# A recommender forward pass: the last block's first layer begun in the counts' PSUM banks, transposes tile by tile, token rows that drift against the counts, and tables split by TensorE

## The chip, the cores and the metric

The kernel runs on one core of one Trainium2 chip. A core has five engines that work side by side, each through its own instructions in order: TensorE (PE, matrix products and transposes into PSUM), VectorE (DVE), ScalarE (ACT), GpSimd (POOL, which here issues the gathers) and SyncE (SP, plain transfers). The metric is the device time in microseconds of one execution. In tables and profiles, PEld is TensorE's loading of weights, which overlaps PE.

## The reference

There are 16384 examples. Each has 32 token indices into a table of 50000 rows of 300 numbers, three lists of 20 indices into smaller tables (1000, 5000 and 10000 rows of 64) and four single indices (tables of 100, 50, 20 and 1000 rows of 64). Rows are averaged or taken, put side by side to 748 features, and passed through three dense layers; a "wide" sum of one number per small index is added at the end.

```python
tok = word_emb[token_idx].mean(axis=1)                 # 32 rows of 300
e1 = emb_mh1[mh1_idx].mean(axis=1)                     # 20 rows of 64; e2, e3 alike
o1 = emb_oh1[oh1_idx]                                  # o2, o3, o4 alike
emb = concatenate([tok, e1, e2, e3, o1, o2, o3, o4], axis=1)
wide = (wide_mh1[mh1_idx].sum(axis=(1, 2)) + ... + wide_oh4[oh4_idx][:, 0])[:, None]
h = relu(emb @ W1 + b1)      # 748 -> 1024
h = relu(h @ W2 + b2)        # -> 512
h = relu(h @ W3 + b3)        # -> 256
return sigmoid(h @ Wd + bd + wide)
```

## The kernel before

The batch is cut into 128 tiles of 128 examples. A tile's **token rows** are gathered by POOL with indirect transfers, one row per example and transfer, 32 transfers a tile, two to a buffer (a "group"); DVE adds them into a sum that lives in PSUM. The sums over the **small tables** are matrix products: for each tile DVE makes one-hot rows, TensorE multiplies them into counts (how often an example uses each of the 128 x 138 table rows), ScalarE moves the counts to SBUF as 8-bit numbers, and TensorE multiplies the counts with the tables, which are held on the chip as three bf16 terms. A tile takes 11 steps of counting; the small sums of tile t run in the steps of tile t + 1. The layers of a block of four tiles (512 examples) are spread over the steps of the next four tiles.

```python
tokp = ctx.enter_context(tc.tile_pool(name="tok", bufs=2 * TOK_LAG))       # TOK_LAG = 3
ps_h = ctx.enter_context(tc.tile_pool(name="ps_h", bufs=2, space=bass.MemoryType.PSUM))
ps_c = ctx.enter_context(tc.tile_pool(name="ps_c", bufs=1, space=bass.MemoryType.PSUM))
... # tables: each part of 23 slices becomes three bf16 terms
            for c in range(3):
                ...
                if c:
                    nc.vector.scalar_tensor_tensor(
                        rows, rows, 2.0 if c == 1 else 1.0, term[c - 1], op0=ALU.mult, op1=ALU.subtract
                    )
                nc.scalar.activation(term[c], rows, AF.Copy, scale=2.0 if c == 0 else 1.0)
                yield 1
... # token rows
    def add_up(t, q, rows):
        a, b = rows[:, 0:TOK_D], rows[:, TOK_D : 2 * TOK_D]
        if q == 0:
            nc.vector.tensor_add(tok_sum, a, b)
        else:
            nc.vector.tensor_add(tok_sum, tok_sum, a)
            to = features[t][:, 0:TOK_D] if q == n_groups - 1 else tok_sum
            nc.vector.tensor_add(to, tok_sum, b)

    def tokens(t, it):
        for q in range(n_groups):
            rows = tokp.tile([P, TOK_GROUP * TOK_D], F32, name="tok_rows")
            for r in range(TOK_GROUP):
                j = q * TOK_GROUP + r
                nc.gpsimd.indirect_dma_start(...)
            under_way.append((t, q, rows))
            if len(under_way) > TOK_LAG:
                add_up(*under_way.pop(0))
            yield 1
... # small sums: by pairs of tables
                    nc.tensor.matmul(
                        pg[:, j, :], by_slice[:, :, h], terms[:, h, :], start=(h == h0), stop=(h == h1 - 1)
                    )
... # features transposed for the layers, 512 examples at a time
    def transposed(x, gs):
        n = len(gs) * P
        for k in range(NK):
            kk = chunk_k[k]
            pt = ps_h.tile([P, BLOCK], F32, name="pt", tag="ph")
            for s, g in enumerate(gs):
                nc.tensor.transpose(pt[:kk, s * P : (s + 1) * P], chunk(g, k), ident)
            nc.vector.tensor_scalar(
                x[:kk, k, 0:n], pt[:kk, 0:n], scale[:kk, k : k + 1], None, ALU.mult
            )
            yield CHUNK_WORK
... # one layer: n_out groups of matmuls, each ended by one ScalarE operation
            ph = ps_h.tile([P, BLOCK], F32, name="ph", tag="ph")
            for k, kk in enumerate(kks):
                nc.tensor.matmul(ph[:, 0:n], weights[:kk, k, m * P : (m + 1) * P], src[:kk, k, 0:n], ...)
            nc.scalar.activation(dst[:, m, 0:n], ph[:, 0:n], AF.Relu, bias=bias[:, m : m + 1])
... # order of the whole
    sizes = [NSUB] * (tiles // NSUB - 1) + [NSUB - 2, 1, 1]
    for t in range(tiles + 1):
        ...
        for i in range(STEPS):                       # 11 steps
            if t < tiles:
                hot = one_hots(...)                  # for the next step
                counts(cnt, hot_now, i)
                tables_on_chip.to(TABLE_PACE * (t * STEPS + i - 2))
                toks.to(n_groups * (i + 1) / STEPS)
            done = next(sums) if sums else 0
            if layers:
                layers.to(...)                       # its share of the step
```

Of the kernel before, what the change touches and what calls it, by code (L numbers as in the profile page):

```python
# [8 lines left out]
F32 = mybir.dt.float32  # L9
# [14 lines left out]
TOK_LAG = 3  # L24
BLOCK = 512
HALF = P // 2
N_SMALL = 3 * N_MH + 4
ONEHOT = 6
STEPS = -(-HALF // ONEHOT)
CHUNK_WORK = 1  # L30
TABLE_PACE = 1.2
LAYER_TIME = 10
# [6 lines left out]
G_COLS = TOK_D + 7 * ROW  # L39
# [7 lines left out]
def kernel(  # L47
# [23 lines left out]
    NSUB = BLOCK // P  # L71
# [5 lines left out]
    for f in SMALL:  # L77
# [4 lines left out]
    tokp = ctx.enter_context(tc.tile_pool(name="tok", bufs=2 * TOK_LAG))  # L82
    const = ctx.enter_context(tc.tile_pool(name="const", bufs=1))
    idxp = ctx.enter_context(tc.tile_pool(name="idx", bufs=2))
# [4 lines left out]
    gp = ctx.enter_context(tc.tile_pool(name="g", bufs=NSUB + 1))  # L89
    wp = ctx.enter_context(tc.tile_pool(name="wide", bufs=2 * NSUB))  # L90
    xp = ctx.enter_context(tc.tile_pool(name="x", bufs=1))
# [8 lines left out]
        [(0, 128)],  # L100
        [(128, 256)],
        [(256, 300), (684, 748)],
        [(300, 428)],
        [(428, 556)],
        [(556, 684)],
    ]
# [7 lines left out]
    scale = const.tile([P, NK], F32, name="scale")  # L114
    nc.vector.memset(scale, 1.0)
    nc.vector.memset(scale[:, 0:2], 1.0 / N_TOK)
    nc.vector.memset(scale[0 : TOK_D - 256, 2:3], 1.0 / N_TOK)
    nc.vector.memset(scale[:, 3:4], 1.0 / N_MH)
    nc.vector.memset(scale[0:EMB, 4:5], 1.0 / N_MH)
# [23 lines left out]
    PART = n_h // 6  # L143

    def load_tables(part0, tag):
        raw = xp.tile([P, PART, ROW], F32, name="raw", tag=tag)
# [14 lines left out]
    def convert_tables():  # L161


        tags = ("even", "odd")
        raws = [load_tables(k * PART, tags[k]) for k in range(2)]
        yield
        for part in range(n_h // PART):
            rows = raws[part]
            if 1 <= part < n_h // PART - 1:
                raws.append(load_tables((part + 1) * PART, tags[(part + 1) % 2]))  # L170
            for c in range(3):
                term = [
                    terms[:, part * PART : (part + 1) * PART, k * ROW : (k + 1) * ROW]
                    for k in range(3)
                ]
                if c:
                    nc.vector.scalar_tensor_tensor(
                        rows, rows, 2.0 if c == 1 else 1.0, term[c - 1], op0=ALU.mult, op1=ALU.subtract
                    )
                nc.scalar.activation(term[c], rows, AF.Copy, scale=2.0 if c == 0 else 1.0)  # L180
                yield 1
# [22 lines left out]
    under_way = []  # L204
    features = {}

    def add_up(t, q, rows):

        a, b = rows[:, 0:TOK_D], rows[:, TOK_D : 2 * TOK_D]
        if q == 0:  # L210
            nc.vector.tensor_add(tok_sum, a, b)  # L211
        else:
            nc.vector.tensor_add(tok_sum, tok_sum, a)  # L213
            to = features[t][:, 0:TOK_D] if q == n_groups - 1 else tok_sum
            nc.vector.tensor_add(to, tok_sum, b)  # L215

    def tokens(t, it):


        for q in range(n_groups):  # L220
            rows = tokp.tile([P, TOK_GROUP * TOK_D], F32, name="tok_rows")
            for r in range(TOK_GROUP):
                j = q * TOK_GROUP + r
                nc.gpsimd.indirect_dma_start(  # L224
                    out=rows[:, r * TOK_D : (r + 1) * TOK_D],
                    out_offset=None,
                    in_=word,
                    in_offset=bass.IndirectOffsetOnAxis(ap=it[:, j : j + 1], axis=0),
                )
            under_way.append((t, q, rows))  # L230
            if len(under_way) > TOK_LAG:
                add_up(*under_way.pop(0))
            yield 1

    def last_tokens():
        for group in under_way:
            add_up(*group)

    def load_indices(blk):
# [15 lines left out]
        return it, ix  # L255
# [309 lines left out]
```

## Time and profile before

| what | before |
|---|---|
| device time, median of 3 | 5270.46 us (5268.77 to 5272.05) |
| span of the profiled run | 5269.3 us |
| mean granted TensorE clock | 0.989 |
| gathers | 4096, busy 3896.4 us, 951 ns each |
| DVE busy | 3768.8 us |
| ScalarE busy | 2447.1 us |
| f32 matmuls of the layers (5984 records) | 1474.1 + 1211.0 us |
| small-table matmuls (17664) | 1849.6 us |
| counts (16384) | 758.4 us |

A line of the profile's list of groups gives source line, engine, operation, output and inputs by the program's names, how often, then busy time and mean length of one in ns, then the engine's idle time just before them and what ended it. A line of the timeline gives start and length in us, the same names, and in brackets the idle time before. In the names, `tok_rows` are gathered token rows, `own` is the PSUM bank with the token sum, `pc` the counts in PSUM, `cnt` the counts in SBUF, `pg` the small sums, `pt` transposes, `ph` a layer's output, `terms` the tables' bf16 terms and `raw` the tables as loaded. L224 is the gather, L388 a layer's matmul, L337 a small-table matmul, L312 a counting matmul, L177 the table subtraction. Busy time of an engine is the time in which an instruction of it is under way; what an engine spends between instructions is not in it.

### The profile page before, as it was taken

What the parts mean: (1) busy time and instruction counts of PE and PEld (TensorE: products, weight loads), DVE (VectorE), ACT (ScalarE), POOL (GpSimd) and SP (SyncE); (2) the same over time, 40 slices, a digit from 0 to 9 for tenths busy, and PEclk for the clock granted to TensorE, in tenths of its full rate; (3) what the DMA queues carried; (4) which work ended last, traced back from release to release, by engine and by line L of the source; (5) the groups of instructions that cost most, each with busy time, mean ns of one, the idle gap of its engine ahead of it and who ended that gap; (6) DMA issues with size and microseconds to landing.
All of it is one profiled execution on the core that took longest, in us unless ns stands there. A gap on an engine that the chain in (4) does not pass through costs nothing.

```text
span 5269.3 us, 104252 instructions
## 1 busy us (share of the span) xinstructions
PE 5094.7 (97%) x41320; PEld 3164.7 (60%) x41320; DVE 3768.8 (72%) x8014; ACT 2447.1 (46%) x1938; POOL 3897.3 (74%) x4103
## 2 busy tenths in 40 slices
PE   4799999999999999999999999999999999999999
PEld 3565656566565656656655656556566566656658
DVE  8777777777777777777777777777777777777752
ACT  5444444444444444444444444444444444444432
POOL 7777777777777777777777777777777777777762
PEclk8899999999999999999999999999999999999999
DMA  6444444444444444444444444444444444444431
GB/s 190 125 125 124 125 125 126 126 125 124 125 125 125 125 124 125 125 125 126 125 124 125 126 125 126 124 125 125 125 125 125 124 126 125 125 125 125 124 103 34
DMA packets 252890, 652.60 MB, mean 124 GB/s; under 512 B 119009, under 2 KB 119524, under 8 KB 252399
## 3 DMA queue, kind: packets, MB, share of 16 engines
q0 software_dynamic: 196608, 629.41, 43.5%
q1 hardware_dynamic: 55791, 16.53, 1.4%
q8 instruction: 323, 5.29, 0.4%
q14 instruction: 168, 1.38, 0.1%
HBM read 645.59 MB, written 0.07 MB: 123 GB/s over the span
## 4 chain that ended last, share of the span: by engine, by line
PE 37%; DMA 23%; DVE 16%; issue 14%; POOL 10%; ACT 0%; DVEq 0%; SPq 0%; POOLq 0%; ACTq 0%
DMA tok_rows<-in_word_emb_dram,it 22%; PE ph L388 20%; PE pg L337 12%; POOL tok_rows L224 10%; DVE own L215 5%; PE pc L312 4%; DVE own L213 3%; DVE slice L294 3%; DVE row L294 2%; DVE x L379 1%; DVE g L343 1%; PE po L413 1%; DVE own L211 0%; DVE g L215 0%; PE po L417 0%
## 5 line engine op out<-in xcount | busy, mean ns | idle before, releaser
L224 POOL DMA_INDIRECT tok_rows<-in_word_emb_dram,it x4096 | 3896.4, 951 | 1293.4 <-issue 755.5
L319 ACT ACTIVATE cnt<-pc 128x1656 fp8e3<-128x1656 f32 (+1 forms) x1408 | 2121.7, 1507 | 2056.4 <-PE pc L312 2026.0
L337 PE MATMUL pg<-terms,cnt 128*128 128x195 bf16 x17664 | 1849.6, 254 | 87.7 <-DVE g L343 86.3
L337 PEld LDWEIGHTS <-cnt 128*128 128x128 fp8e3 x17664 | 1601.3, 144 | 234.6 <-issue 81.1
L388 PE MATMUL ph<-x,w_sb 128*128 128x512 f32 (+5 forms) x3264 | 1474.1, 581 | 4.2 <-DVE x L379 3.5
L215 DVE TENSOR_TENSOR own<-own,tok_rows 128x300 f32<-128x300 f32 x1792 | 857.7, 479 | 680.6 <-DMA tok_rows<-in_word_emb_dram,it 647.3
L388 PE MATMUL ph<-h,w_sb 128*128 128x512 f32 (+2 forms) x2720 | 1211.0, 573 | 0.0
L213 DVE TENSOR_TENSOR own<-own,tok_rows 128x300 f32<-128x300 f32 x1920 | 918.8, 479 | 387.6 <-DMA tok_rows<-in_word_emb_dram,it 335.8
L312 PEld LDWEIGHTS <-row 64*128 64x128 bf16 x16384 | 501.7, 95 | 1041.3 <-DVE own L215 246.1
L294 DVE TENSOR_TENSOR row<-own,sc 128x768 bf16<-128x768 bf16 (+1 forms) x1408 | 762.4, 541 | 162.8 <-PE pc L312 89.5
L312 PE MATMUL pc<-slice,row 64*128 64x138 bf16 x16384 | 758.4, 224 | 70.6 <-DVE slice L294 36.7
L388 PEld LDWEIGHTS ph<-x,w_sb 128*128 128x128 f32 (+1 forms) x3264 | 564.3, 194 | 414.6 <-issue 401.9
L294 DVE TENSOR_TENSOR slice<-own,sc 128x828 bf16<-128x828 bf16 (+1 forms) x1408 | 797.9, 567 | 0.0
L388 PEld LDWEIGHTS ph<-h,w_sb 128*128 128x128 f32 x2720 | 463.3, 192 | 317.9 <-issue 316.0
L397 ACT ACTIVATE h<-ph,b_sb 128x512 f32<-128x512 f32 (+2 forms) x476 | 316.3, 665 | 683.2 <-PE ph L388 678.2
L343 DVE TENSOR_REDUCE g<-pg 128x130 f32<-128x390 f32 (+1 forms) x512 | 259.2, 506 | 151.1 <-PE pg L337 150.8
L379 DVE TENSOR_SCALAR x<-pt,scale 128x512 f32<-128x512 f32 (+4 forms) x204 | 137.0, 712 | 3.7 <-PE pt L378 2.9
L378 PE MATMUL pt<-ident,g 128*128 128x128 f32 (+1 forms) x768 | 104.1, 275 | 3.0 <-DVE x L379 2.5
L211 DVE TENSOR_TENSOR own<-tok_rows 128x300 f32<-128x300 f32 x128 | 61.4, 480 | 49.5 <-DMA tok_rows<-in_word_emb_dram,it 47.3
L378 PEld LDWEIGHTS pt<-ident,g 128*128 128x128 f32 (+1 forms) x768 | 85.5, 141 | 7.7 <-DVE x L379 6.7
L215 DVE TENSOR_TENSOR g<-own,tok_rows 128x300 f32<-128x300 f32 x128 | 60.2, 471 | 22.3 <-DMA tok_rows<-in_word_emb_dram,it 18.3
L413 PE MATMUL po<-h,wd_sb 128*1 128x512 f32 (+2 forms) x136 | 60.9, 566 | 0.3
(34 smaller groups left out, 290.1 us busy)
## 6 DMA issues: line engine op xcount, KB each, us to landing
tok_rows<-in_word_emb_dram,it POOLq DMA_INDIRECT x4096
ix<-in_idx_dram SPq DMA_DIRECT2D x128, 32.0 KB
w_sb<-in_W_dram SPq DMA_DIRECT2D x6, 512.0 KB
raw<-in_mh_dram SPq DMA_DIRECT2D x3, 747.5 KB
it<-in_idx_dram SPq DMA_DIRECT2D x32, 64.0 KB
w_sb<-in_W_dram SPq DMA_DIRECT2D x1, 2048.0 KB
raw<-in_mh_dram SPq DMA_DIRECT2D x1, 617.5 KB
out_dram<-h SPq DMA_DIRECT2D x31, 2.0 KB
```

The costliest lines, as they stand in the source:

```text
L213: nc.vector.tensor_add(tok_sum, tok_sum, a)
L215: nc.vector.tensor_add(to, tok_sum, b)
L224: nc.gpsimd.indirect_dma_start(out=rows[:, r * TOK_D : (r + 1) * TOK_D], out_offset=None, in_=word, in_offset=bass.IndirectOffsetOnAxis(ap ...
L294: nc.vector.tensor_tensor(one[:, 0:rows, :].rearrange("p i (n d) -> p i n d", d=2), iota[:, 0:n].rearrange("p (n d) -> p n d", d=2).unsque ...
L312: nc.tensor.matmul(pc[:, f, k // n, at : at + n_h], hot[0][half, k, :], hot[1][half, k, :], start=True, stop=True,)
L319: nc.scalar.activation(cnt[:, :, b : b + rows, :].rearrange("l f (g k) h -> l f g (k h)", g=2), pc[:, :, :, 0 : n * n_h], AF.Copy, scale=0 ...
L337: nc.tensor.matmul(pg[:, j, :], by_slice[:, :, h], terms[:, h, :], start=(h == h0), stop=(h == h1 - 1))
L343: nc.vector.tensor_reduce(g[:, at : at + n * ROW].rearrange("p (f d) -> p f d", f=n), pg[:, 0:n, :].rearrange("p f (c d) -> p f d c", c=3) ...
L378: nc.tensor.transpose(pt[:kk, s * P : (s + 1) * P], chunk(g, k), ident)
L379: nc.vector.tensor_scalar(x[:kk, k, 0:n], pt[:kk, 0:n], scale[:kk, k : k + 1], None, ALU.mult)
L388: nc.tensor.matmul(ph[:, 0:n], weights[:kk, k, m * P : (m + 1) * P], src[:kk, k, 0:n], start=(k == 0), stop=(k == len(kks) - 1),)
L397: nc.scalar.activation(dst[:, m, 0:n], ph[:, 0:n], AF.Relu, bias=bias[:, m : m + 1])
```

## The change

Five things change together. (1) The tables' second and third bf16 terms are no longer made by subtracting on DVE: TensorE adds the raw table and minus one half of the terms made so far in PSUM, seven slices at a time, and ScalarE copies the difference out. (2) Blocks of the layers hold two tiles (256 examples) and not four, with two blocks of one tile at the end. The features of a tile are transposed as soon as they are there: the small ones and the token sums each by themselves, into tiles of their own; the wide sum rides along as a row of one of the transposes and is added by DVE, where TensorE added it with a matmul per tile. (3) The token rows have one queue for the whole batch, spread over all steps and 16 more (WAKE), so that a tile's rows may come in later than its counts; there are eight buffers for them and not six. (4) For the last tile the part of the first layer that needs no token sum is done early for four of its eight outputs, in the PSUM banks which the counts no longer need. (5) The pacing follows: a block's layers are spread from when its features are ready until those of the next block will be.

```diff
-TABLE_PACE = 1.2
-LAYER_TIME = 10
+TOK_BUFS = 8
+WAKE = 16
+EARLY = 3
+LAYER_TILES = 2
+SPLIT = 7
+PART = 3 * SPLIT
+TABLE_PACE = 1.3
+LAYER_TIME = 2.5
...
+        def make(p, c):
+            if c == 0:
+                nc.scalar.activation(term(p, 0), rows(p), AF.Copy, scale=2.0)
+                return
+            _, a, b = pieces[p]
+            left = ps_h.tile([P, SPLIT, ROW], F32, name="left", tag="ph")[:, 0 : b - a, :]
+            nc.tensor.matmul(left, ident, rows(p), start=True, stop=False)
+            for k in range(c):
+                nc.tensor.matmul(left, minus_half, term(p, k), start=False, stop=(k == c - 1))
+            nc.scalar.activation(term(p, c), left, AF.Copy, scale=2.0)
...
+    n_all = B // P * n_groups + TOK_LAG
+    def tokens():
+        under_way = []
+        for n in range(n_all):
+            if n < n_all - TOK_LAG:
+                t, q = divmod(n, n_groups)
...
+            if n >= TOK_LAG:
                 add_up(*under_way.pop(0))
             yield 1
...
+        def add_small(self, t, g):
+            at = self.columns(t)
+            pt = ps_h.tile([P, 4, P], F32, name="pt", tag="ph")
+            nc.tensor.transpose(pt[:, 3, :], g[:, 0:P], ident)
+            for k in range(3):
+                c = (1 + 2 * k) * ROW + 1
+                nc.tensor.transpose(pt[:, k, :], g[:, c : c + P], ident)
+            nc.vector.tensor_tensor(self.small[:, 0:3, at], pt[:, 0:3, :], scale..., ALU.mult)
+            nc.vector.tensor_copy(self.small[0:EMB, 3, at], pt[0:EMB, 3, :])
+            nc.vector.tensor_copy(self.wide[:, at], pt[EMB : EMB + 1, 3, :])
+        def add_tokens(self, t, g):
...
+            for k in range(2):
+                nc.tensor.transpose(pt[:, k, :], g[:, k * P : (k + 1) * P], ident)
+            nc.tensor.transpose(pt[0 : EMB + rest, 2, :], g[:, TOK_D - rest - EMB : TOK_D], ident)
...
+    def early_part(block):
+        part = ps_c.tile([P, 4, 512], F32, name="pc")
+        for m in range(4):
+            for k in range(NK - 3):
+                nc.tensor.matmul(part[:, m, 0 : block.n], w1_sb[...], block.chunk(k), start=(k == 0), stop=False)
...
-        for s, wide in enumerate(wides):
-            nc.tensor.matmul(
-                po[:, s * P : (s + 1) * P], wide, ident, start=False, stop=(s == len(wides) - 1)
-            )
+        nc.vector.tensor_add(y, po[:, 0:n], block.wide[:, 0:n])
...
-    sizes = [NSUB] * (tiles // NSUB - 1) + [NSUB - 2, 1, 1]
+    n_steps = tiles * STEPS + WAKE
+    sizes = [LAYER_TILES] * (tiles // LAYER_TILES - 1) + [1] * LAYER_TILES
...
+        toks.to(n_all * (step + 1) / n_steps)
...
+        if step == n_steps - EARLY:
+            part = early_part(block_of[tiles - 1])
```

## The prediction

> **What bounds the kernel now.** I read the page's table of engines first: it points at TensorE (97% busy) and gives GpSimd 74%. The busy time by stage, read next (columns: stretch, its length, busy us and instructions of PE, PEld, DVE, ACT, POOL, then clock and DMA), says something else.
>
> ```profile
> PE 5094.7 (97%) x41320; PEld 3164.7 (60%) x41320; DVE 3768.8 (72%) x8014; ACT 2447.1 (46%) x1938; POOL 3897.3 (74%) x4103
> ```
>
> ```profile
> 100.00:125.00 25.00, 15.51 (x189) 13.04 (x187) 18.95 (x39) 12.17 (x8) 18.90 (x21) 0.84 0.46 124
> ...
> 2000.00:3000.00 1000.00, 985.36 (x7967) 601.91 (x7966) 730.89 (x1557) 468.69 (x367) 756.67 (x799) 0.99 0.46 125
> 3000.00:4000.00 1000.00, 986.01 (x7966) 602.21 (x7964) 727.62 (x1549) 469.25 (x368) 756.96 (x798) 0.99 0.46 125
> ```
>
> POOL does the same 798 or 799 gathers in every thousand microseconds, and about as many per us (21 in 25 us) before any layer runs and PE is a third idle. The timeline of POOL alone shows why: a gather starts every 1.25 us, 0.95 busy and 0.30 of its own overhead, whatever the view puts in brackets.
>
> ```profile
> 2499.57 0.95 POOL L224 DMA_INDIRECT tok_rows<-in_word_emb_dram,it  x1 [0.30 <-issue]
> 2500.82 0.95 POOL L224 DMA_INDIRECT tok_rows<-in_word_emb_dram,it  x1 [0.31 <-DVE own L213]
> 2502.07 0.95 POOL L224 DMA_INDIRECT tok_rows<-in_word_emb_dram,it  x1 [0.30 <-issue]
> ```
>
> So the gathers are the bound: 4096 x 1.2535 us (1000 us over 797.8) = 5134 us. The first starts at 3.1 us and the last ends at 5191.3, so POOL lost 5191.3 - 3.1 - 5134 = 54 us. Two places hold it. At the start, twelve table subtractions on DVE each hold one gather up; below, the gather that starts at 25.16 takes 2.09 us, because it can only proceed when the subtraction of 24.72 ends at 26.43.
>
> ```profile
> 24.72 1.71 DVE L177 SCALAR_TENSOR_TENSOR raw<-raw,terms 128x1495 f32<-128x1495 f32 x1
> ...
> 25.16 2.09 POOL L224 DMA_INDIRECT tok_rows<-in_word_emb_dram,it  x1 [0.30 <-issue]
> ```
>
> Twelve gathers are longer than 1.3 us, all so placed; together 11 us over 0.95 each. The rest, 43 us, falls after 5050 us: PE runs the two-tile block squeezed into one tile's steps, DVE follows PE, and gathers wait for buffers.
>
> ```profile
> 5153.54 0.95 POOL L224 DMA_INDIRECT tok_rows<-in_word_emb_dram,it  x1 [5.35 <-DVE g L215]
> ...
> 5163.70 0.54 PE L312 MATMUL pc<-slice,row 64*128 64x138 bf16 x12
> 5164.18 1.51 PE L337 MATMUL pg<-terms,cnt 128*128 128x195 bf16 x15
> 5165.53 3.65 PE L388 MATMUL ph<-x,w_sb 108*128 108x256 f32 x16
> 5169.11 0.54 PE L312 MATMUL pc<-slice,row 64*128 64x138 bf16 x12
> 5169.59 1.52 PE L337 MATMUL pg<-terms,cnt 128*128 128x195 bf16 x15
> 5170.94 4.08 PE L388 MATMUL ph<-x,w_sb 128*128 128x256 f32 x18
> ```
>
> A step there is 5.4 us (counts at 5163.70, then at 5169.11), the next 5.8, against 40.1 / 11 = 3.65 in the middle. After the last gather PE still works 78 us, to 5269.3: the rest of that block and two blocks of one tile. Thus 5269.3 = 3.1 + 5134 + 11 + 43 + 78.
>
> PE is the near second. In the middle a tile takes 32 x 1.2535 = 40.1 us, PE is busy 0.985 of it: 39.5 us. It begins the layers only after step 57, at 224 us.
>
> [...] POOL is full at 74 to 76%. [...] The trace has each f32 matmul as two records whose starts lie 429 ns apart at 512 columns, 216 at 256 and 112 at 128 (read in the tail)[...], and halving N costs almost nothing.
>
> **The change part by part.**
>
> *Tables split by TensorE.* Twelve DVE subtractions of 1.71 us go: POOL gets back 11 us. In their place PE does 40 f32 matmuls (ident x raw, 455 columns at most: 2 x 0.385 us) and 60 bf16 ones (about 0.2 us): 31 + 13 = 44 us within steps 3 to 19. ScalarE makes 60 terms of 455 columns instead of 18 of 1495; between 0.37 (128 columns) and 0.69 us (512) one takes about 0.63. Per step that is 1.3 pieces: PE 1.3 x 2.2 = 2.9, with counts (0.6) and, from step 11, sums (1.2) some 4.7 us; ScalarE 1.55 + 1.3 x 1.9 = 4.0. POOL's pace is 3.6. Over 17 steps the lag comes to 15 to 20 us, more while the clock is halved (the 0.84 above). Eight buffers less the lag of three let POOL run 12.5 us ahead, so I charge 8 us. Net gain at the start: 3 us.
>
> *Blocks of two tiles, transposed tile by tile.* The first ph matmul comes after 34 steps' counts instead of 57. Matmuls per tile: 88 records of 216.4 ns instead of 44 of 430: +0.13 us. Transposes 7 instead of 6 (+0.11), no wide matmuls (2 x 0.109 less), two more switches from f32 to bf16 (0.096 each, from 525 against 429 ns between starts): together +0.21, so 39.7 us a tile, all on PE's path. From the built order, PSUM banks are taken so that only 16 of 619 ph-after-ph reuses follow within 1 us; no new wait of size. DVE gains about 0.7 us a tile of small copies (75 to 80% busy, beside other work); ScalarE 0.48 us twice for 0.69: beside other work.
>
> *Drifting token rows.* The 2048 groups plus 3 are spread over 1424 steps instead of tile by tile over 1408: 1.4403 groups a step, 2.507 us each: 3.611 us a step, 39.7 a tile. POOL stays full, counts run ahead of it, and when the last row lands only one tile's layers are left. PE's need is 39.7 too: the two bounds meet, and PE has nothing to spare.
>
> *The end.* Block 124-125 gets 11 steps, then 126 alone, 127 begun early in the counts' banks. PE's built order, priced by start-to-start times of this trace (pg 0.0875, a switch from f32 0.096 more), leaves after step 1393: 308 pg 28 us, 128 f32 matmuls of 256 columns 57, 176 of 128 columns 40, counts 7, transposes and output 5: 137 us, the last block's 17.5 among them. By then DVE has added group 1.4403 x 1394 - 3 = 2005, which landed at about 3.1 + 2006 x 2.507 + 5.8 (1.25 issue, 4.5 in flight as the chain of waits shows) = 5038, with the 8 us above 5046. Then 137, layer-boundary bubbles of about 3, and 2.4 from the last matmul to the end (5266.9 to 5269.3 now): 5188. POOL alone would allow 5137 + 8 for the last gather, 5 to land, 1 of adding, 1 of transposing, 18 of layers, 3 to store: 5173. PE sets the end by some 15 us.
>
> The sum against now: 54 us of POOL losses become about 8 at the start plus about 10 at the end, and 78 after the last gather become about 33: 5269 - 36 - 45 = 5188.
>
> **Rivals.** (1) *PE becomes the bound throughout.* For it: 39.7 against 39.7, and short half-clock windows (mean granted clock 0.99) cost it about 0.2 us a tile. Against: when PE is late DVE no longer waits for rows, so the 86 us that PE now waits before pg for DVE's reductions (the waits view) should shrink. A tile of 40.0 us for 125 tiles gives 5188 + 35 = 5225. (2) *Everything is hidden and POOL is the only bound:* no loss at the start, the tail squeezed: 5137 + 28 = 5165, the floor. (3) *Two ph buffers with transposes in between make PE wait for ScalarE:* a wait of 0.8 us at each of 256 insertions is +200, 5390; the bank order read above speaks against it. (4) *Nothing gained because PE was the bound all along:* the layers start 23 steps earlier but the work is the same; PE's idle time before the layers, 9.5 of 25 us in the first line above, would be the only gain: 23 steps x 3.65 x 0.38 = 32 us, less 44 of splitting: 5281. POOL's constant spacing speaks against it.
>
> **Range and chances.** Main sum 5188; (2) draws it to 5165, (1) to 5225. 80%: 5163 to 5222. Faster by 2% needs under 5165.0, the floor itself: 0.10. Slower by 2% needs (3): 0.02. Within 2%: 0.88.
>
> **What would show it.** Right: gathers 1.25 us apart to the end, none stretched to 2 us in the first 80 us; last gather ending near 5150 to 5160; less than 40 us after it; tiles 39.7 to 40 us apart; matmuls of 256 columns 216 ns apart. Wrong: gathers waiting for buffers in the middle (PE binds), a gather pace that is not 1.25, PE waiting for ScalarE before ph, or a start that loses more than 20 us while TensorE splits tables.

## The result and the profile after

| | before | after |
|---|---|---|
| device time, median of 4 | 5271.26 us (5268.77 to 5273.40) | 5193.97 us (5193.00 to 5194.77) |
| ratio | 1 | 0.9853, 95% interval 0.9836 to 0.9871 |
| span of the profiled run | 5269.3 us | 5191.3 us |
| start and end of the first and last gather | 3.1 and 5191.3 us | 3.1 and 5149.5 us |
| from the last gather's end to the end of all | 78.0 us | 41.8 us |
| last counting matmul starts | 5202.7 us | 5097.8 us |

The change saves 77 us, 1.5%: within 2%, as predicted, and 6 us above the 5188 of the prediction. In the kernel after, L255 is the gather, L461 a layer's matmul, L365 a small-table matmul, L340 a counting matmul, L305 the transposes of the key columns, L407 and L410 those of small features, L426 and L427 those of token sums, L470 ScalarE's reading of a layer's output, and L237, L239 and L243 the additions of token rows. `pk` are transposed key columns (the small indices from which the one-hot rows are made), `wide_row` the wide sums, `x_small` and `x_tok` transposed features, `g_tok` a tile's finished token sum. The table of engines of the kernel after, and below it the busy time by stage (stretch, its length, busy us and instructions of PE, PEld, DVE, ACT, POOL, then clock, DMA share and GB/s):

```profile
PE 5113.7 (99%) x46912; PEld 4177.5 (80%) x46912; DVE 3890.9 (75%) x8502; ACT 2600.7 (50%) x2445; POOL 3888.4 (75%) x4103
```

```profile
100.00:125.00 25.00, 15.41 (x208) 12.79 (x202) 23.57 (x49) 13.50 (x9) 18.90 (x21) 0.96 0.45 124
2000.00:3000.00 1000.00, 988.98 (x9103) 808.40 (x9103) 756.19 (x1648) 500.84 (x463) 756.76 (x799) 1.00 0.46 125
3000.00:4000.00 1000.00, 992.94 (x9182) 813.20 (x9181) 762.36 (x1661) 505.69 (x465) 757.02 (x798) 1.00 0.46 125
```

POOL still does 798 or 799 gathers in a thousand microseconds. TensorE has no slack left: 989 to 993 busy, where it had 985. DVE has some 30 us more to do per thousand and hides it. POOL's timeline in the middle, and at the place where the table subtractions stood:

```profile
24.54 0.95 POOL L255 DMA_INDIRECT tok_rows<-in_word_emb_dram,it  x1 [0.30 <-DMA tok_rows<-in_word_emb_dram,it]
25.79 0.94 POOL L255 DMA_INDIRECT tok_rows<-in_word_emb_dram,it  x1 [0.30 <-issue]
...
2499.84 0.95 POOL L255 DMA_INDIRECT tok_rows<-in_word_emb_dram,it  x1 [0.30 <-issue]
2501.09 0.95 POOL L255 DMA_INDIRECT tok_rows<-in_word_emb_dram,it  x1 [0.30 <-issue]
```

No gather in the first 80 us is stretched: the first takes 1.10 us, the others 0.95 at most. What is lost lies in three waits: 1.2 us at 89.6, and the two near the end that the timeline of POOL shows here, 2.0 and 7.4 us beyond the usual 0.30.

```profile
5109.85 0.95 POOL L255 DMA_INDIRECT tok_rows<-in_word_emb_dram,it  x1 [2.29 <-DVE own L243]
...
5134.82 0.95 POOL L255 DMA_INDIRECT tok_rows<-in_word_emb_dram,it  x1 [7.75 <-DVE own L243]
```

The chain that ended last, before and then after:

```profile
PE 37%; DMA 23%; DVE 16%; issue 14%; POOL 10%; ACT 0%; DVEq 0%; SPq 0%; POOLq 0%; ACTq 0%
```

```profile
PE 94%; DVE 2%; issue 1%; DMA 1%; ACT 0%; POOL 0%; SPq 0%; DVEq 0%; ACTq 0%
```

Before, it runs over POOL, the transfers and DVE; after, over TensorE almost alone. The waits of TensorE say what changed hands, again before and then after. A line of waits gives who waited for whom, the sum in us, how often, and the longest:

```profile
PE pg L337 <- DVE g L343: 86.3, 95, 3.3
PE pc L312 <- DVE slice L294: 36.7, 33, 4.1
PE pc L312 <- ACT cnt L319: 33.9, 16, 5.2
```

```profile
PE pk L305 <- DVE wide_row L415: 32.0, 28, 1.2
PE pc L340 <- DVE slice L322: 9.0, 8, 2.4
PE pg L365 <- DVE g L371: 7.6, 10, 2.1
```

The waits for DVE's reductions have shrunk from 86.3 to 7.6 us, as rival 1 said they should if TensorE is late. A wait that was not there has come: `pk`, the transposes of the next four tiles' key columns.

One measure tells which bound holds: how far apart the tiles lie, from ScalarE's first copy of counts of tile 10 to that of tile 110, over 100. It is compared with what the gathers alone would allow: 32 x 1.2535 = 40.11 us a tile before. With the drift, 2051 groups of two gathers (2048 and the lag of 3) go to 1424 steps, and a tile has 11 steps: 11 x 2051 / 1424 x 2 x 1.2535 = 39.72 us.

| kernel | tile 10 | tile 110 | us per tile | gathers alone |
|---|---|---|---|---|
| before | 414.87 | 4423.44 | 40.09 | 40.11 |
| after | 403.16 | 4380.19 | 39.77 | 39.72 |

Before, the steps go at the gathers' pace. After, they are 0.05 us a tile slower than the gathers would allow, some 6 us over 120 tiles, by which POOL's lead of eight buffers shrinks before it meets the waits above at the end. So small a difference does not decide by itself which engine sets the pace. Experiments 5 and 6 do: on a chip whose gathers would allow 39.65 us, the tiles lie 39.77 us apart again, so it is TensorE.

### The profile page after: what moved, and what is told of

Same layout as the page of the kernel before. It is cut to its first block, busy times and chain, and to the rows that moved or that the text cites. A ratio compares the mean times of both kernels' runs of the same rounds, so it can differ in the third digit from the quotient of the medians.

```text
span 5191.3 us, 116518 instructions
## 1 busy us (share of the span) xinstructions
PE 5113.7 (99%) x46912; PEld 4177.5 (80%) x46912; DVE 3890.9 (75%) x8502; ACT 2600.7 (50%) x2445; POOL 3888.4 (75%) x4103
## 4 chain that ended last, share of the span: by engine, by line
PE 94%; DVE 2%; issue 1%; DMA 1%; ACT 0%; POOL 0%; SPq 0%; DVEq 0%; ACTq 0%
PE ph L461 46%; PE pg L365 32%; PE pc L340 12%; PE po L486 1%; PE pt L426 1%; PE pt L410 1%; PE pt L407 1%; DMA tok_rows<-in_word_emb_dram,it 1%; DVE own L239 1%; DVE own L243 0%; DMA w_sb<-in_W_dram 0%; POOL tok_rows L255 0%; DVE slice L322 0%; PE left L194 0%; PE pt L427 0%
## 5 line engine op out<-in xcount | busy, mean ns | idle before, releaser
L255 POOL DMA_INDIRECT tok_rows<-in_word_emb_dram,it x4096 | 3887.5, 949 | 1260.5 <-issue 873.6
L365 PE MATMUL pg<-terms,cnt 128*128 128x195 bf16 x17664 | 1828.7, 253 | 7.9 <-DVE g L371 7.6
L365 PEld LDWEIGHTS <-cnt 128*128 128x128 fp8e3 x17664 | 1590.3, 144 | 162.1 <-issue 31.8
L461 PE MATMUL ph<-h,w_sb 128*128 128x256 f32 (+1 forms) x5200 | 1224.2, 379 | 0.5 <-ACT h L470 0.5
L461 PE MATMUL ph<-x_small,w_sb 128*128 128x256 f32 (+2 forms) x4128 | 1044.4, 381 | 4.8 <-DVE x_small L429 3.0
L461 PEld LDWEIGHTS ph<-h,w_sb 128*128 128x128 f32 x5200 | 930.8, 191 | 99.2 <-issue 0.8
L239 DVE TENSOR_TENSOR own<-own,tok_rows 128x300 f32<-128x300 f32 x1920 | 917.0, 478 | 63.3
L243 DVE TENSOR_TENSOR own<-own,tok_rows 128x300 f32<-128x300 f32 x1792 | 856.8, 478 | 61.8
L340 PEld LDWEIGHTS <-row 64*128 64x128 bf16 x16384 | 495.4, 94 | 484.8 <-issue 227.5
L470 ACT ACTIVATE h<-ph,b_sb 128x256 f32<-128x256 f32 (+1 forms) x906 | 426.8, 471 | 912.3 <-PE ph L461 912.0
L461 PEld LDWEIGHTS ph<-x_small,w_sb 128*128 128x128 f32 (+1 forms) x4128 | 739.3, 191 | 86.6 <-PE ph L461 6.4
L340 PE MATMUL pc<-slice,row 64*128 64x138 bf16 x16384 | 751.0, 223 | 15.8 <-DVE slice L322 9.0
L461 PE MATMUL ph<-x_tok,w_sb 128*128 128x256 f32 (+1 forms) x2064 | 565.4, 380 | 0.0
L461 PEld LDWEIGHTS ph<-x_tok,w_sb 128*128 128x128 f32 x2064 | 373.0, 192 | 40.9
L428 DVE TENSOR_SCALAR x_tok<-pt 128x256 f32<-128x256 f32 x128 | 54.4, 425 | 301.6 <-PE pt L427 301.6
L411 DVE TENSOR_TENSOR x_small<-pt,scale 128x384 f32<-128x384 f32 x128 | 71.2, 556 | 91.8 <-PE pt L410 91.8
L486 PE MATMUL po<-h,wd_sb 128*1 128x256 f32 (+1 forms) x260 | 68.0, 374 | 1.6 <-DVE x_small L429 1.0
```

The source lines that it names most:

```text
L255: nc.gpsimd.indirect_dma_start(out=rows[:, r * TOK_D : (r + 1) * TOK_D], out_offset=None, in_=word, in_offset=bass.IndirectOffsetOnAxis(ap ...
L340: nc.tensor.matmul(pc[:, f, k // n, at : at + n_h], hot[0][half, k, :], hot[1][half, k, :], start=True, stop=True,)
L365: nc.tensor.matmul(pg[:, j, :], by_slice[:, :, h], terms[:, h, :], start=(h == h0), stop=(h == h1 - 1))
L411: nc.vector.tensor_tensor(self.small[:, 0:3, at], pt[:, 0:3, :], scale.unsqueeze(2).to_broadcast([P, 3, P]), ALU.mult)
L461: nc.tensor.matmul(ph[:, 0:n], weights[: src.shape[0], k, m * P : (m + 1) * P], src, start=(k == 0), stop=(k == len(srcs) - 1),)
L486: nc.tensor.matmul(po[:, 0:n], wd_sb[:, k : k + 1], h3[:, k, 0:n], start=(k == 0), stop=(k == M3 - 1))
```

## The experiments

Where a ratio is given, it is to the kernel before, timed beside it. Chips differ a little in the gathers' pace (1.2535 us in the two profiles above, 1.2507 to 1.2512 where nothing is in the way on the chips of the six experiments), so the kernel before takes 5260 to 5271 us. Where the gathers set the time, as in the kernel before and in experiments 1 to 4, the ratio is taken to carry over from chip to chip: the kernel before itself took 5261.4 us on one of these chips and 5271.3 on that of the change, 0.998 of it, as 1.2508 is of 1.2535. Where TensorE sets it, as in the kernel after and in experiments 5 and 6, where the tiles lie 39.77 us apart on both chips, the time itself is, and is compared there.

**1. Did the gathers bound the kernel before?** Half of layer 2's products are left out, in the kernel before.

```diff
-        yield from layer(h2, w2_sb, b2_sb, h1, [P] * M1, M2, n)
+        yield from layer(h2, w2_sb, b2_sb, h1, [P] * (M1 // 2), M2, n)
...
-    mlp_time = (NK * (CHUNK_WORK + M1) + M1 * M2 + M2 * M3 + M3) * LAYER_TIME
+    mlp_time = (NK * (CHUNK_WORK + M1) + M1 // 2 * M2 + M2 * M3 + M3) * LAYER_TIME
```

> The kernel before, with half of layer 2's products left out (the inner sum runs over 4 of the 8 column chunks of h1, so its output is not the reference's): 64 of 128 products of 512 columns and their second records less per block of four tiles, about 440 us of TensorE work in the whole run. Meant for a chip on which the kernel before takes some 5270 us. If the gathers bound the kernel before: about 5240, since only the buffer waits (43 us) and part of the end (78 us) can go. If TensorE bounds it: 5270 - 440 = some 4830, until the gathers' floor of about 5150 stops it, so 5150 to 5165. A result of 5225 to 5250 speaks for the gathers, one of 5150 to 5165 for TensorE.

Of the 32 products in layer 2 of a block, 16 are left out; the expectation's 64 of 128 is a miscount, its 440 us is not (32 records of 0.43 us in each of some 32 blocks). Measured: 5233.91 us against 5261.4, ratio 0.9947 (0.9930 to 0.9963). The stages in the middle:

```profile
2000.00:3000.00 1000.00, 924.93 (x7792) 575.62 (x7786) 729.01 (x1559) 471.51 (x368) 756.61 (x800) 0.97 0.47 125
3000.00:4000.00 1000.00, 920.66 (x7787) 574.26 (x7788) 726.57 (x1552) 471.24 (x368) 756.61 (x800) 0.97 0.46 125
```

TensorE's share fell to 92%, and POOL did its 800 gathers as before. Of some 440 us of work taken from TensorE, 27 us reached the end, all from the last stretch: the last gather ended at 5165.0, and 68 us followed. (In the profile before they are 5191.3 and 78; 9 us of the first difference are the chip, 4096 x 0.0023.) The gathers were the bound.

**2. Without the drift.** The kernel after, with the token rows paced over the 1408 steps of the counts.

```diff
-        return max(-(-(n_groups * (t + 1) + TOK_LAG) * n_steps // n_all) + 1, (t + 2) * STEPS + 1)
+        return max(-(-(n_groups * (t + 1) + TOK_LAG) * tiles * STEPS // n_all) + 1, (t + 2) * STEPS + 1)
...
-        toks.to(n_all * (step + 1) / n_steps)
+        toks.to(n_all * (step + 1) / (tiles * STEPS))
```

> The kernel after with the token rows paced over the 1408 steps of the counts, without the drift over the 12 extra steps. Numbers for a chip where the kernel before takes 5260 to 5270. Theory (the gathers are the floor and TensorE is only just beside them; without the drift the gathers must keep step with the tiles, and the 12 steps' worth of token adds is squeezed in ahead): VectorE's waits for rows come back (over 300 us idle for rows) and pass on to TensorE as waits for the reduced groups; 5195 to 5215, ratio 0.987 to 0.990. Rival (drift does nothing, since TensorE and the gathers are level either way): ratio 0.9853, as the kernel after. Second rival (without drift the steps end earlier and so does the whole): ratio under 0.983.

Measured: 5242.02 us against 5260.52, ratio 0.9965 (0.9949 to 0.9982). On the chip of the kernel after that is 59 us behind it (0.9965 - 0.9853 = 0.0112 of 5271). On this chip, with faster gathers, it is about 48 us (5242.0 - 5194.0, an estimate which takes the kernel after to need the same time here, as experiments 5 and 6 suggest). The direction is the theory's; the time lies 27 us above the most that it allowed. (The drift left out is the 16 steps of WAKE; the expectation's 12 is a slip.) Its waits of DVE:

```profile
DVE own L243 <- DMA tok_rows<-in_word_emb_dram,it: 454.8, 692, 3.0
DVE own L239 <- DMA tok_rows<-in_word_emb_dram,it: 226.1, 317, 2.2
DVE g L371 <- PE pg L365: 154.8, 122, 18.4
```

DVE waits for rows again, as in the kernel before. The tiles lie 40.11 us apart, on the pace of the gathers. And the gathers hardly wait: the last ends at 5131.6. What was mis-sized is what follows it: 107.9 us. The last counting matmul starts at 5147.6, against 5097.8 in the kernel after. So without the drift every step of counting waits for its share of rows, and the counts, sums and layers of the last tiles are left over when the rows are in. With it the counts are 16 steps ahead at the end, and that work lies beside the gathers. The drift is most of the change's gain; all the rest together is worth the 18.5 us between this version and the kernel before.

**3. The wait for the key columns.** In the kernel after the key columns of the next four tiles are transposed in the second step of every fourth tile. A tile's small features are often transposed in the same step, just before, and TensorE then waits until DVE has emptied the PSUM bank, 28 times and 32.0 us in all. The timeline of TensorE in the kernel after shows one:

```profile
1042.68 0.33 PE L407 MATMUL pt<-ident,g 128*128 128x128 f32 x1
1042.85 0.49 PE L410 MATMUL pt<-ident,g 128*128 128x128 f32 x3
1044.47 0.40 PE L305 MATMUL pk<-ident_bf,keys 128*128 128x128 bf16 x4 [1.14 <-DVE wide_row L415]
1044.71 1.47 PE L365 MATMUL pg<-terms,cnt 128*128 128x195 bf16 x15
```

Moved to a step that holds no transposes of features:

```diff
+        moved = False
         if waiting and step >= waiting[0][0]:
+            moved = True
             block = transpose(*waiting.pop(0)[1:])
...
-        if s == 2 and i == 1 and t + NSUB < tiles + 1:
-            next_sc = key_columns(next_keys)
+        if s == 2 and i >= 1 and next_keys is not None and not moved:
+            next_sc, next_keys = key_columns(next_keys), None
```

> The kernel after with one change: the next tile's key columns are transposed in a step that holds no transposes of token features, so TensorE doesn't wait for VectorE to empty the bank between the two (31 waits of some 1.3 us in the kernel after). Numbers for a chip where the kernel before takes 5260 to 5270. Theory (the waits ate TensorE's slack, and it is the late steps of TensorE that hold the last token buffers and the end): with 38 us of TensorE time back, its steps fall back to the gathers' pace, the two buffer waits at the end (10 us) shrink to some 3 us, and the end after the last gather stays at 42 us, for the begun outputs still wait for ScalarE: 0.983 to 0.9845 of the kernel before. Rival (the gain of the version with both changes came from the begun outputs alone): the ratio of the kernel after, 0.9853.

Measured: 5172.99 us against 5260.52, ratio 0.9831 (0.9815 to 0.9847), as the theory had it; the interval just overlaps that of the kernel after, so the ratio alone doesn't part them. If the medians hold, some 12 of the 32 us of waits came off (0.0022 of 5271), and the gathers hide the rest. The trace parts the two. The wait before `pk` is gone, and the tiles lie 39.59 us apart, where the gathers of this chip allow 39.63 (11 x 2051 / 1424 x 2 x 1.2507; 4 us over the 100 tiles are within the lead of the buffers). TensorE waits for DVE's reductions again, here in its waits, so POOL is the bound again. POOL waits longer than its 0.3 us only once near the end, here in its timeline:

```profile
PE pg L365 <- DVE g L371: 23.1, 39, 1.9
```

```profile
5115.89 0.94 POOL L255 DMA_INDIRECT tok_rows<-in_word_emb_dram,it  x1 [3.22 <-DVE own L243]
```

The last gather ends at 5130.6, and the 41.8 us behind it are the same as in the kernel after.

**4. The end: begun outputs.** The four outputs begun early share one PSUM tile. TensorE's timeline in the kernel after shows what follows from it, once the last token sum is there:

```profile
5162.83 0.44 PE L426 MATMUL pt<-ident,g_tok 128*128 128x128 f32 x2 [1.26 <-DVE g_tok L243]
5163.11 0.27 PE L427 MATMUL pt<-ident,g_tok 128*108 128x128 f32 x1
5164.20 0.49 PE L461 MATMUL pc<-x_small,w_sb 108*128 108x128 f32 x2 [0.83 <-DVE x_small L429]
5164.53 1.00 PE L461 MATMUL pc<-x_tok,w_sb 128*128 128x128 f32 x4
5166.04 0.79 PE L461 MATMUL pc<-x_small,w_sb 108*128 108x128 f32 x2 [0.51 <-ACT h L470]
5166.62 1.06 PE L461 MATMUL pc<-x_tok,w_sb 128*128 128x128 f32 x4
5168.14 0.80 PE L461 MATMUL pc<-x_small,w_sb 108*128 108x128 f32 x2 [0.46 <-ACT h L470]
5168.73 1.06 PE L461 MATMUL pc<-x_tok,w_sb 128*128 128x128 f32 x4
5170.25 0.80 PE L461 MATMUL pc<-x_small,w_sb 108*128 108x128 f32 x2 [0.46 <-ACT h L470]
```

Each next output waits until ScalarE has read the one before it, though it is another part of that tile (0.51, 0.46 and 0.46 us); and matmuls of four records take 1.06 us where 0.61 is usual, for the granted clock is 0.50, here in the busy time by stage:

```profile
5164.60:5174.80 10.20, 8.78 (x38) 7.90 (x38) 0.00 (x0) 1.77 (x5) 0.00 (x0) 0.50 0.00 0
```

In this version all four are completed first and then read, on top of experiment 3:

```diff
-        for m in range(n_out):
-            begun = part is not None and m < 4
+        m0 = 0
+        if part is not None:
+            m0 = 4
+            for m in range(4):
+                for k in range(NK - 3, NK):
+                    nc.tensor.matmul(part[:, m, 0:n], ..., start=False, stop=(k == NK - 1))
+            for m in range(4):
+                nc.scalar.activation(dst[:, m, 0:n], part[:, m, 0:n], AF.Relu, bias=bias[:, m : m + 1])
+        for m in range(m0, n_out):
```

> The kernel after, with two changes: the next tile's key columns are transposed in a step that holds no transposes of token features (so TensorE doesn't wait for VectorE to empty the bank between the two, some 31 waits of about 1.3 us), and the begun outputs of the last block are completed by TensorE first, all four, before ScalarE reads any of them (so three waits of about 0.5 us go, and the TensorE clock need not drop). Theory (TensorE and the gathers nearly meet, and what TensorE waits for in the middle only eats its slack): the gathers stay the floor, so 5180 to 5190 on a chip where the kernel after takes 5194. Rival (TensorE alone is the bound in the middle): the 38 us of waits come off whole, 5150 to 5160. Second rival (neither wait is on the path that sets the end): 5192 to 5196.

Measured: 5168.61 us against 5261.4, ratio 0.9824 (0.9808 to 0.9841). This is the fastest version measured. The time lies below the theory's range and above the rival's, and that needs reading. Of the 25 us between the spans (5191.3 and 5166.2) about 11 are the chip: 4096 gathers at 1.2508 instead of 1.2535 us. On the chip of the kernel after this version would by that estimate lie near 5180, the lower end of the theory's range and well above the rival's 5150 to 5160. The last gather ends at 5130.6, as in experiment 3, and 35.6 us follow instead of 41.8. TensorE's timeline shows where the 6 us went:

```profile
5143.91 0.44 PE L426 MATMUL pt<-ident,g_tok 128*128 128x128 f32 x2 [1.26 <-DVE g_tok L243]
5144.18 0.27 PE L427 MATMUL pt<-ident,g_tok 128*108 128x128 f32 x1
5145.28 0.49 PE L460 MATMUL pc<-x_small,w_sb 108*128 108x128 f32 x2 [0.82 <-DVE x_small L429]
5145.60 0.61 PE L460 MATMUL pc<-x_tok,w_sb 128*128 128x128 f32 x4
5146.05 0.39 PE L460 MATMUL pc<-x_small,w_sb 108*128 108x128 f32 x2
5146.27 0.61 PE L460 MATMUL pc<-x_tok,w_sb 128*128 128x128 f32 x4
```

From the last token transposes to the end it takes 22.3 us (5143.9 to 5166.2), against 28.5 (5162.8 to 5191.3) in the kernel after. The waits on ScalarE sum to 1.4 us; the rest is the clock, which stays at 1.00 here (10.2 us at 0.50 cost about 5, an estimate: half of 10.2). It had fallen in the kernel after before the first of these waits (the four records at 5164.53 take 1.00 us), so the waits did not start it. Whether they kept it low is open: it stayed at half for 10.2 us in the kernel after and in experiments 3 and 6, which have them, and for 3.4 us in experiment 5, which has none; but in experiment 2 the same waits came, 2.4 us in all, and the clock stayed at 1.00.

**5. Without the early part.** The kernel after, with the last block's first layer made whole behind the last token transposes:

```diff
         if step == n_steps - EARLY:
-            part = early_part(block_of[tiles - 1])
+            part = None
```

> The kernel after with one part undone: the last block's first layer is not begun ahead in the counts' PSUM banks; its 4 outputs are made whole behind the last token transposes, as the other 4. Numbers for a chip where the kernel before takes 5260 to 5270; the kernel after had a ratio of 0.9853. Theory (the begun outputs share one PSUM tile, so TensorE waits 3 times for ScalarE at the very end, and its clock drops there; that costs what the 24 records of 0.11 us begun ahead save): within 4 us of the kernel after to either side, ratio 0.9845 to 0.986. Rival (the part does what it is for): its 24 records and the order of the work come back, +5 to +9 us, ratio 0.9863 to 0.987.

Measured: 5188.74 us against 5261.38, ratio 0.9861 (0.9845 to 0.9878). The ratio lies a hair above the theory's range, but theory and rival both took the kernel after's ratio as the yardstick, and it does not carry over to this chip: the tiles lie 39.77 us apart where the gathers would allow 39.65 (11 x 2051 / 1424 x 2 x 1.2512), so TensorE sets the time. In time this version is 5 us faster than the kernel after's 5193.97, just beyond the theory's 4 and against the rival. The end of its trace agrees. TensorE's timeline at the last token transposes:

```profile
5163.60 0.69 PE L426 MATMUL pt<-ident,g_tok 128*128 128x128 f32 x2 [2.51 <-DVE g_tok L243]
```

They wait longer than in the kernel after, since the early matmuls ahead of them are gone, so the ends are best counted from the start of the last counting matmul: 93.5 us with the early part as the change has it (93.6 in experiment 3), 89.2 without it (from 5099.7), 87.3 with it when no output waits for ScalarE (experiment 4). So the part the change is named for costs about 4 us as it is written. Completed as in experiment 4, it ends 2 us earlier than without it. Of these 2, some 1.7 are the half clock that experiment 5 has for 3.4 us (an estimate: half of 3.4), so that the early matmuls save time by themselves is not shown.

**6. Tables on DVE again.** The kernel after, with the tables' terms made by subtractions on DVE, as in the kernel before. There are fourteen here, of 1365 columns at most, where the kernel before (and the expectation) has twelve of 1495:

```diff
-            nc.tensor.matmul(left, ident, rows(p), start=True, stop=False)
-            for k in range(c):
-                nc.tensor.matmul(left, minus_half, term(p, k), start=False, stop=(k == c - 1))
-            nc.scalar.activation(term(p, c), left, AF.Copy, scale=2.0)
...
+                if c:
+                    nc.vector.scalar_tensor_tensor(
+                        rows, rows, 2.0 if c == 1 else 1.0, term[c - 1], op0=ALU.mult, op1=ALU.subtract
+                    )
+                nc.scalar.activation(term[c], rows, AF.Copy, scale=2.0 if c == 0 else 1.0)
```

> The kernel after with the tables' terms split by VectorE again (12 operations, as in the kernel before), once more, for a chip where the kernel before takes 5260 to 5270. Theory (the gathers are the floor from the first to the last): each of the 12 operations holds a gather back by about 1 us, and TensorE's 44 us less give nothing back: +8 to +12 us over the kernel after, ratio 0.987 to 0.988. Rival (TensorE sets the steps, and the gathers catch up through the buffers): TensorE's 44 us less count, 0 to -20 us, ratio 0.981 to 0.985.

Measured: 5196.92 us against 5261.38, ratio 0.9877 (0.9860 to 0.9893). The ratio fits the theory, but here too it is the time that can be compared: 3 us above the kernel after's 5193.97, where the theory had 8 to 12. The trace speaks against the theory's reason too. The stretched gathers are back, here DVE's and then POOL's timeline:

```profile
25.63 1.57 DVE L180 SCALAR_TENSOR_TENSOR raw<-raw,terms 128x1365 f32<-128x1365 f32 x1
...
26.02 1.99 POOL L235 DMA_INDIRECT tok_rows<-in_word_emb_dram,it  x1 [0.30 <-DVE slice L302]
```

How far behind this kernel's gathers were can be read against experiment 5, which ran on the same chip with the tables on TensorE: the 65th gather starts at 92.5 us against 83.3, the 1001st at 1263.5 against 1257.6, the 3001st at 3768.8 against 3766.5; the last ends at 5153.6 against 5151.4. Nine microseconds have become two. In both kernels the tiles lie 39.77 us apart, on a chip whose gathers would allow 39.65, so TensorE sets the steps, and gathers that start late catch up. The two profiled spans differ by 6.4 us (5195.3 and 5188.9): 2.2 have come by the last counting matmul (5101.9 and 5099.7), and 4.2 follow it, which are the early part that experiment 5 leaves out.

**On other chips.** Six runs fell on two chips on which the kernel before takes 7120 us, 35% more, and where what bounds it is something else. The edits of four of them are those of experiments 1, 2, 3 and 6. `b1` is the kernel before with the tables split by TensorE alone, that part of the change by itself; on a chip of the usual kind it has no run.

> The kernel before with the tables split by TensorE, nothing else. If the gathers are the bound: no gather of the first 100 us longer than 1.3 us, the last gather ends about 5180 instead of 5191, the end moves with it by 10 to 11 us, to about 5260. If TensorE is the bound: its 44 us more of work show as 0 to +40 us, 5270 to 5310.

7127.31 us, ratio 1.0007 (0.9990 to 1.0024).

> The kernel before with half of the second layer's products left out (its input features 512 to 1023), 16 of 88 f32 matmuls per block, about 3.4 us of TensorE per tile, 440 us in all. If the gathers are the bound: tiles in the middle stay 40.1 us apart, only the tail behind the counts shrinks, 15 to 40 us less, about 5240. If TensorE is the bound: 350 to 440 us less, about 4870.

7019.18 us, ratio 0.9859 (0.9840 to 0.9878).

> The changed kernel with the token rows paced over the 1408 steps of the counts, without the 16 steps of drift. If the gathers are the bound: a step costs 3.646 us of gathers again and not 3.611, the counts end 40 to 50 us later, and the small sums and two blocks of layers follow the last gather: 5220 to 5235. If TensorE alone sets the time, the pace of the rows does not matter: 5190 to 5200.

7500.39 us, ratio 1.0540 (1.0512 to 1.0568).

> The changed kernel with the transposes of the index keys moved to a step in which no features are transposed, so that they no longer wait for VectorE to empty the PSUM bank just filled (31 waits of about 1.3 us in the trace, 38 us). If TensorE is the bound in the middle: up to 38 us less, stopped by the gathers' floor, 5165 to 5175. If the gathers are the bound there and TensorE only at the end: 0 to 5 us less, 5189 to 5194.

7562.79 us, ratio 1.0620 (1.0597 to 1.0643).

> The kernel after with one part undone: the tables' three terms are split by VectorE again, with the 12 operations of the kernel before, instead of by TensorE. Numbers for a chip where the kernel before takes 5260 to 5270; the kernel after had a ratio of 0.9853 to it. Theory (the gathers are the floor from the first to the last; each of the 12 operations holds a gather back by about 1 us): 11 us come back at the start, of which TensorE's 44 us less in the steps 3 to 19 give nothing back, so +8 to +12 us, ratio 0.987 to 0.988. Rival (TensorE sets the steps and the gathers catch up through the buffers): TensorE has 44 us less to do, so 0 to -20 us, ratio 0.981 to 0.985.

7549.10 us, ratio 1.0610 (1.0583 to 1.0636).

> The kernel before with one part of the change alone: the tables' terms are split by TensorE, through the identity and minus a half of it. Numbers for a chip where the kernel before takes 5260 to 5270. Theory (the gathers are the floor): the 11 us by which 12 gathers are stretched in the first 80 us go, and the buffer waits behind 5050 us don't grow by as much, so -4 to -11 us, ratio 0.998 to 0.9993. Rival (TensorE is the bound, and the 44 us go onto it): ratio 1.002 to 1.008.

7135.88 us, ratio 1.0031 (1.0005 to 1.0056).

None of these tests the theories it was made for, since all of them reckon with gathers that follow each other every 1.25 us. On these chips gathers that need not wait still start about 1.25 us apart (four in a row from 28.00 to 31.76 us in the second run of `b1`), but many wait for buffers: the mean spacing is 1.72 us in the second run of `b1` and 1.83 in that of the tables on DVE, whose waits head this list ("remote" is an end that the profile can't lay to an instruction of this core):

```profile
POOL tok_rows L235 <- DVE own L223: 2262.4, 649, 17.2
ACT cnt L327 <- remote: 1527.5, 297, 13.1
DVE row L302 <- remote: 1271.4, 232, 11.5
```

The granted clock is 0.88 to 0.91, which by estimate, dividing by 0.9, would make TensorE's 5100 us some 5700 (it is busy 5683 and 5891 us in the two) and not 7100. Waits like these fill the rest; what causes them is not shown. Three forms of the changed kernel took 5 to 6% more than the kernel before there. The kernel after itself did not run on such a chip, so that it would lose there is likely and not shown; nor is it shown why. The second run of `b1` shows one thing that does carry over: its longest gather takes 1.10 us (the mean is 0.945, where the kernel before has 0.951), so without the subtractions none is stretched there either.

## Why the prediction held, and where it did not

The prediction's sum against the profile of the kernel after:

| term | predicted, us | measured, us |
|---|---|---|
| first gather, 4096 x 1.2535 | 3 + 5134 | 3.1 + 5134 |
| lost at the start | 8 | 1.2 |
| small stretches on the way | 0 | 1.8 |
| waits for buffers at the end | 10 | 9.4 |
| after the last gather | 33 | 41.8 |
| sum | 5188 | 5191.3 |

The sum is the span; the time itself lies 2.7 us above it, which the prediction left out. Two terms failed in opposite directions and cancelled, so that the sum came within 3 us is in part luck. Of the signs named in advance, the pace of the gathers, the unstretched start and the distance of the tiles came. The end did not: 41.8 us where less than 40 was to show that the prediction is right.

*The gathers bound the kernel before:* right, by experiment 1 (27 us of 440).

*Tables split by TensorE, "net gain at the start: 3 us":* the stretched gathers went, as said. The charge of 8 us for TensorE's 44 us was too high; one wait of 1.2 us came. Its prices held: from start to start an f32 record of 455 columns mostly takes 0.38 us and a bf16 one 0.20, and ScalarE takes 0.55 to 0.58 for a term, where 0.63 was reckoned. Yet what is saved at the start is hardly on the path to the end any more: experiment 6 hands back 9 us at the start and 2 at the end.

*"No new wait of size" in the blocks of two tiles:* wrong. The reading of the bank order looked at ph after ph, and passed over pk after pt: 28 waits, 32 us, all TensorE's. The need of 39.7 us a tile was 39.77, against 39.72 for the gathers; less these waits (32 us over 128 tiles, 0.25 each) it would be about 39.5 by estimate, so this term too was met by two errors against each other.

*"The two bounds meet":* right, and closer than could be said in advance. TensorE is the slower, by 0.05 us a tile here and by 0.12 on the chip of experiments 5 and 6, so rival 1 was true in kind; its 5225 did not come because a tile takes 39.77 us and not the 40.0 it feared. The half-clock windows that rival 1 priced at 0.2 us a tile (between 1000 and 4000 us of the kernel before nine of 3.4 us at 0.50) are gone: from 130 to 5164 us of the kernel after the granted clock is 1.00.

*The drift:* the mechanism is right ("when the last row lands only one tile's layers are left"), and experiment 2 puts 59 us on it (48 on its own chip). The prediction gave it no price of its own: that most of the gain hung on it was not seen.

*The end, "the last block's 17.5":* mis-sized for this kernel. From its first matmul with token features to TensorE's last it took 24.3 us (5164.2 to 5188.5) through the shared PSUM tile and the clock. It takes 18.1 (5145.3 to 5163.4, experiment 4) when neither is in the way.

*What of the blocks of two tiles and the tile-by-tile transposes was worth how much by itself* was not tried; 77 us less the 59 of the drift leaves some 18 for all the rest, if the parts add up.

*The stretched gathers:* the twelve of the kernel before took 1.39 to 2.49 us, and each ended 0.82 us after the subtraction beside it, wherever it had begun. Experiment 6 agrees: the subtraction of 25.63 ends at 27.20, and the gather of 26.02 at 28.01, 0.8 us later. Why the two collide is not shown.

*The clock at the end* was not foreseen: it was 0.50 for 10.2 us here and for 3.4 in experiment 5. TensorE's waits just before are 1.26 and 0.83 us here; in experiment 4 the clock was 1.00 at the same place behind waits of 1.26 and 0.82 us, so the gaps alone do not decide it. What does is not shown.

## What to carry to other kernels

Where two engines are level, price a change by what it leaves to do after the last item of the bound has gone by, and let the bound's own work drift against the rest so that this remainder is small; here that was worth more than all the other parts together. Before claiming that a rearrangement brings no new wait, list every pair of neighbours that use the same buffer, not only those of the kind in mind. And a result that agrees with its prediction still deserves the term-by-term comparison: here two errors of 7 and 9 us hid one another, and the larger one led to the faster version.

## What the runs showed that was not expected

Indirect gathers were held up by an ordinary addition too. DVE's first addition of a tile (L237, 0.48 us) has both inputs in SBUF, and gathers that started soon after its start were stretched, here in the timeline of the kernel after:

```profile
2340.27 0.48 DVE L237 TENSOR_TENSOR own<-tok_rows 128x300 f32<-128x300 f32 x1
2340.34 1.22 POOL L255 DMA_INDIRECT tok_rows<-in_word_emb_dram,it  x1 [0.31 <-issue]
```

It ends 0.81 us after the addition, as the gather of experiment 6 ended 0.81 us after the subtraction. In the kernel after, 24 gathers take over 1.05 us where 0.95 is usual, and 22 of them overlap such an addition: 21 begin 0.06 to 0.21 us after its start (they take 1.08 to 1.23 us), one begins 0.05 us before it (1.32), and all end 0.81 or 0.82 us after it. The kernel before has 14 of the kind (1.09 to 1.24 us). Additions with one input in PSUM (L239, L243) are 30 times as many, and none of the 1460 gathers that begin within one takes over 0.96 us. The gathers' pace differed between chips by 0.2% (1.251 and 1.2535 us). And two of the chips took 34 to 46% longer for each kernel that was run on both kinds, in a way that turned a gain of 1.5% into losses of 5 to 6% for close relatives of the changed kernel.
